# Block transposes on VectorE and two new matmul tilings in the first part of a conv-attention-MoE kernel

## The chip, the cores and the metric

The kernel runs on one core of a Trainium2 chip. The metric is the device time of one execution in microseconds (us); lower is better. Before the change the median of three runs is 6059.13 us (6056.47 to 6059.99).

A core has five engines with queues of their own, which run side by side and wait for one another by semaphores: PE (TensorE, matmuls; its weight loads are listed as PEld), DVE (VectorE), ACT (ScalarE), POOL (GpSimd) and SP (SyncE, which issues most transfers). Data lies in SBUF (128 partitions) and, for matmul results, in PSUM. Transfers between the chip's memory and SBUF are carried by 16 DMA engines. A matmul holds one operand in the array (its weights: contraction rows by output columns) and streams the other through it (the moving columns). The array can be split into tiles, for example four of 64 rows by 64 columns or four of 32 rows by 128 columns.

## The reference

`x` has the shape (32, 128, 64, 64): 32 images of 128 channels, 64 by 64 pixels, all in float32. Layer 0 adds to x a convolution in a transformed space: GroupNorm, a complex butterfly transform along H and along W, a product over channels with the transformed weights, and the inverse transforms. Layer 1 is an attention over channels and a mixture of eight experts with two chosen per pixel.

```python
def tensor_product(x, tw1, tw2, increasing_stride):
    y = jnp.swapaxes(butterfly_lastdim(jnp.swapaxes(x, -1, -2), tw1, increasing_stride), -1, -2)
    return butterfly_lastdim(y, tw2, increasing_stride)

def _kop2d(x, weight, kd1, kd2, k11, k12, k21, k22):
    xc = x.astype(jnp.complex64)
    wc = weight.astype(jnp.complex64)
    x_f = tensor_product(xc, _c(k11), _c(k12), False)
    w_f = tensor_product(wc, _c(kd1), _c(kd2), False) * math.sqrt(H * W)
    prod = jnp.einsum('bihw,oihw->bohw', x_f, w_f)
    out = tensor_product(prod, _c(k21), _c(k22), True)
    return jnp.real(out)
...
x = x + _L0_conv_ref(_gn(x), ...)
t = _to_tokens(x)
t = t + _L1_attn_ref(_ln_t(t), ...)
t = t + _L1_ffn_ref(_ln_t(t), ...)
```

The change touches only `x_f`: the GroupNorm of x and its transform along W and H. A butterfly along 64 points is a 64 x 64 complex matrix; the kernel computes the matrices once and multiplies.

## The kernel before

The kernel has three parts, one after the other. The first part takes each image through GroupNorm and the two input transforms and stores the spectrum `xf` (image, channel, w, real and imaginary h). The second part goes over the 64 columns w, mixes channels with the transformed weights and stores `pf`. The third part takes each image back, adds it to x, and does the attention and the experts.

In the first part, image b passes these steps; the names are the planner's keys and the tiles of the profile.

- `load` (L308): eight pieces of 256 KB from `x` into one of three x buffers, on SP's queue. `stats` (L315) takes the statistics of each piece on DVE. `group_norm` (L322) averages them over channel groups with two small matmuls on PE (L332, L342; tile `gps`) and small DVE steps between; `scaled` (L355) normalizes x in place in four pieces, on ACT for the first four images and on DVE after that.
- `turn_over` (L367, tile `pz`): 32 PE transposes of 128x128 per image, in four groups of eight; `turned` (L376): 16 ACT copies of 64x512 from PSUM (L383) write `z` as (w and channel half, channel, h).
- `along_w` (L389, tile `pv`): the W stage, eight groups of 32 matmuls. A matmul has 64 rows, 64 columns (all h of one channel) and 64 moving columns (`pw`, real or imaginary); four tiles of the array are used in turn. `w_out` (L402) copies each group from PSUM to `v` on ACT (L407).
- `along_h` (L413, tile `pf`): the H stage, eight groups of eight matmuls of 128 rows (h, real and imaginary), 128 columns (channels) and 128 moving columns (`ph`). `h_out` (L424) copies each group to an `f` tile, six of eight on DVE and two on ACT (L428).
- `store` (L431): two transfers of 256 KB per group, each from all 128 partitions of `f`, on SP's queue (L436).

PSUM is one pool of four tiles of two banks ("ps"), used in turn by all PE groups. There are two `z`, two `v` and four `f` buffers.

The order of the instructions is not written by hand. `Plan` (L25) simulates the engines before the kernel is built: each step has an engine, a cost in us, a due time in slots of 27.5 us (`SLOT`, L171), the steps that it comes after, and the rooms (buffers) that it takes and frees. On each engine the earliest due step that is ready and whose rooms are free goes next; the instructions are issued in that order, and each engine executes its queue in order. On PE the first part's steps keep the order in which they are added: in slot s and quarter g, the transposes of image s, two W groups of image s-1, two H groups of image s-2; the two GroupNorm matmuls of image s+1 stand before and after one quarter's W groups.

At the start DVE computes the input transform's matrices in six butterfly levels (`level`, L210) from an identity (`unit`, L198, whose copy at L204 sorts rows by parity for this layout) and copies them to `pw` and `ph` (`input_matrices`, L230).

In the second part `weights` (L617, L632; tile `g`) uses four tiles of the array of 32 rows (9 filled) by 128 columns with 128 moving columns, and takes two rooms of one kind at once; `mix` (L645, L654) follows it in turn. The second part's store (L673) reads 64 partitions.

Of the kernel before, what the change touches and what calls it, by code (L numbers as in the profile page):

```python
# [24 lines left out]
class Plan:  # L25
# [12 lines left out]
    def run(self):  # L38
# [12 lines left out]
        while True:  # L51
            for e, heap in ready.items():
                if busy[e]:
                    continue
                passed = []
                while heap:
                    due, i = heapq.heappop(heap)
                    take = ops[i][5]
                    if all(room[k] > 0 for k in take):
                        for k in take:  # L60
                            room[k] -= 1
                        order.append(i)
                        busy[e] = True
                        heapq.heappush(events, (now + ops[i][1], 0, i))
                        break
                    passed.append((due, i))
                for p in passed:
                    heapq.heappush(heap, p)
# [22 lines left out]
def kernel(  # L91
# [39 lines left out]
    pw = cp.tile([P, 2, n], F32, name="pw")  # L131
    ph = cp.tile([P, 2, n], F32, name="ph")
# [30 lines left out]
    with ExitStack() as ph1:  # L163
        pp = ph1.enter_context(tc.tile_pool(name="pp1", bufs=4, space=PSUM))
        xp = ph1.enter_context(tc.tile_pool(name="xp1", bufs=3))
        st = ph1.enter_context(tc.tile_pool(name="st1", bufs=1))
        bp = ph1.enter_context(tc.tile_pool(name="bp", bufs=1))
# [3 lines left out]
        SLOT = 27.5  # L171
# [26 lines left out]
        def unit(m, eng):  # L198
            def run():
                cur = tile_of["bf", m] = bp.tile([P, 2, n], F32, tag="bf", bufs=2, name=f"bf{m}_in")  # L200
                eng.tensor_tensor(cur[:, 0, :], ident[:, 0:n], ident[:, n : 2 * n], ALU.add)
                if m == 1:

                    eng.tensor_copy(  # L204
                        cur[lo, 0, :].rearrange("p (k r) -> p r k", r=2), ident[lo, 0:n].rearrange("p (r k) -> p r k", r=2)
                    )
                eng.memset(cur[:, 1, :], 0.0)
# [22 lines left out]
        def input_matrices():  # L230
            xa = tile_of["bf", 1]
            for half in (lo, hi):
                nc.vector.tensor_copy(pw[half], xa[hi])
            nc.vector.tensor_copy(ph[lo], xa[lo])
            nc.vector.tensor_copy(ph[hi, 1, :], xa[lo, 0, :])
            nc.vector.tensor_scalar_mul(ph[hi, 0, :], xa[lo, 1, :], -1.0)
# [130 lines left out]
        def turn_over(b, g):  # L367
            def run():
                ps = tile_of["pz", b, g] = pp.tile([P, 2, 512], F32, tag="ps", name=f"pz{b}_{g}")
                pv = ps.rearrange("w u (k c) -> w (u k) c", c=P)  # L370
                for k in range(8):
                    h = 2 * (8 * g + k)
                    nc.tensor.transpose(pv[:, k, :], xs[b][:, h * n : (h + 2) * n], ident)  # L373
            return run

        def turned(b, g, r):  # L376

            def run():
                if g == 0 and r == 0:
                    zs[b] = zp.tile([P, n, n], F32, tag="z", name=f"z{b}")  # L380
                pv = tile_of["pz", b, g].rearrange("w u (k c) -> w (u k) c", c=P)
                for half in range(2):
                    nc.scalar.copy(  # L383
                        zs[b][half * n : (half + 1) * n, :, 32 * r + 8 * g : 32 * r + 8 * g + 8],
                        pv[r * n : (r + 1) * n, :, half * n : (half + 1) * n].rearrange("w h c -> w c h"),
                    )
            return run

        def along_w(b, g):  # L389
            def run():  # L390
                ps = tile_of["pv", b, g] = pp.tile([P, 2, 512], F32, tag="ps", name=f"pv{b}_{g}")
                for k in range(8):
                    for half in range(2):
                        rows = slice(half * n, (half + 1) * n)
                        for r in range(2):
                            nc.tensor.matmul(  # L396
                                ps[r * n : (r + 1) * n, half, k * n : (k + 1) * n],
                                zs[b][rows, 8 * g + k, :], pw[rows, r, :], start=True, stop=True,
# [3 lines left out]
        def w_out(b, g):  # L402

            def run():
                if g == 0:
                    vs[b] = vp.tile([P, n, P], F32, tag="v", name=f"v{b}")
                nc.scalar.copy(  # L407
                    vs[b].rearrange("h w (a c) -> h w a c", a=2)[:, :, :, 8 * g : 8 * g + 8],
                    tile_of.pop(("pv", b, g)).rearrange("h a (c w) -> h w a c", w=n),
# [3 lines left out]
        def along_h(b, g):  # L413
            def run():
                ps = tile_of["pf", b, g] = pp.tile([P, 2, 512], F32, tag="ps", name=f"pf{b}_{g}")
                pl = ps.rearrange("c u m -> c (u m)")
                for j in range(8):
                    nc.tensor.matmul(  # L418
                        pl[:, j * P : (j + 1) * P], vs[b][:, 8 * g + j, :], ph.rearrange("h r m -> h (r m)"),
                        start=True, stop=True,  # L420
                    )
            return run

        def h_out(b, g):  # L424
            def run():
                f = tile_of["f", b, g] = fp.tile([P, 8, 2 * n], F32, tag="f", name=f"f{b}_{g}")
                copy = nc.scalar.copy if g % 4 == 3 else nc.vector.tensor_copy
                copy(f.rearrange("c w m -> c (w m)"), tile_of.pop(("pf", b, g)).rearrange("c u m -> c (u m)"))  # L428
            return run

        def store(b, g):  # L431
            def run():
                f = tile_of.pop(("f", b, g))

                for k in range(0, 8, 4):
                    nc.sync.dma_start(xf[b, :, 8 * g + k : 8 * g + k + 4, :], f[:, k : k + 4])  # L436
# [20 lines left out]
        def piece_of_image(b, k):  # L457
# [3 lines left out]
                [("pz", b - 3, g) for g in range(4)] + [("x", b, k - 1), ("pf", b - 4, k)],  # L461
# [28 lines left out]
        def piece(kind, b, g, at):  # L490
            if not 0 <= b < B:
                return
            if kind == "pz":
                add(
                    ("pz", b, g), "PE", 1.0, at, turn_over(b, g), [("nm", b, k) for k in range(4)],
                    ("ps",), ("x",) if g == 3 else (),
                )
                for r in range(2):
                    add(
                        ("zo", b, g, r), "ACT", 1.2, at, turned(b, g, r),  # L500
                        [("pz", b, g)] + [("pv", b - 2, k) for k in range(8)] + ([("zo", b, 0, 0)] if g or r else []),
                        (), ("ps",) if r else (),
                    )
            elif kind == "pv":
                add(
                    ("pv", b, g), "PE", 1.12, at, along_w(b, g),
                    [("zo", b, k, r) for k in range(4) for r in range(2)] + ["wi"], ("ps",),
                )
                add(
                    ("vo", b, g), "ACT", 1.02, at, w_out(b, g),  # L510
                    [("pv", b, g)] + [("pf", b - 2, k) for k in range(8)] + ([("vo", b, 0)] if g else []), (), ("ps",),
                )
            else:
                add(("pf", b, g), "PE", 1.95, at, along_h(b, g), [("vo", b, k) for k in range(8)], ("ps",))
                on_act = g % 4 == 3
# [9 lines left out]
        for s in range(B + 2):  # L525
            if s == 0:
                norm(2)
            for g in range(4):
# [3 lines left out]
                piece("pz", s, g, at)  # L532
                for k in range(2):
                    piece("pv", s - 1, 2 * g + k, at + 0.04 + 0.04 * k)
# [909 lines left out]
```

## Time and profile before

| | |
|---|---|
| median of three runs | 6059.13 us |
| profiled execution, its span | 6062.4 us |
| first part | 0 to 931 us |
| second part | 932 to about 2550 us |
| third part | to the end |
| PE busy over the span | 5891.6 us (97%) |
| DVE, ACT, POOL busy | 4221.2 (70%), 3756.5 (62%), 4191.0 us (69%) |

The profiled execution is its own run, 3.3 us from the median. In the page's groups and in the answers on the trace, a line reads: source line, engine, operation, output tile <- input tiles, shapes, number of records, then busy us and the mean ns of one. Matmuls overlap in the array, so the mean of one matmul is longer than the time from one start to the next; a float32 matmul has two records.

Stretches of the first part (columns: stretch in us, its length, then busy us and records of PE, PEld, DVE, ACT and POOL, the granted PE clock, the DMA engines' share and GB/s):

```profile
0.00:28.00 28.00, 6.86 (x36) 6.48 (x36) 20.94 (x91) 9.20 (x11) 3.07 (x14) 1.00 0.73 253
28.00:65.00 37.00, 24.71 (x714) 22.93 (x715) 15.59 (x33) 35.42 (x49) 1.99 (x6) 0.77 0.21 67
65.00:150.00 85.00, 83.41 (x2043) 80.00 (x2042) 46.81 (x67) 61.78 (x83) 28.51 (x80) 1.00 0.72 237
700.00:900.00 200.00, 198.35 (x4976) 190.43 (x4978) 102.83 (x140) 135.12 (x186) 12.81 (x20) 1.00 0.65 221
```

PE is busy less in the first 65 us, in which the first images pass the steps one after the other, and nearly all of the time from then on.

### The profile page before, as it was taken

The page shows a single profiled execution, that of the slowest core. Times are in us where ns is not written, and L with a number is a line of the kernel's source. Part 1 is how long each engine was busy: PE and PEld are TensorE (multiplying, and loading weights), DVE is VectorE, ACT ScalarE, POOL GpSimd, SP SyncE. Part 2 cuts the span into 40 slices and gives each one's busy share as a digit, 9 for nine tenths or more (in the row PEclk, how much of TensorE's full clock was granted, in tenths as well). Part 3 has the DMA queues.
Part 4 walks back from the last instruction along what each step waited for, and adds up shares of the span by engine and source line. Part 5 has one row for each costly group of instructions (what it writes and reads, how often), then busy time and mean ns, then how long its engine had stood idle before and what let it go on. Part 6 is the DMA issues. An engine that isn't in the chain of part 4 may idle for free.

```text
span 6062.4 us, 219265 instructions
## 1 busy us (share of the span) xinstructions
PE 5891.6 (97%) x95372; PEld 4677.6 (77%) x95372; DVE 4221.2 (70%) x7696; ACT 3756.5 (62%) x7057; POOL 4191.0 (69%) x3765
## 2 busy tenths in 40 slices
PE   7999999999999999889999999999999999999998
PEld 7999999999999999776666666666666666666654
DVE  5565545555555555448878787787878878787878
ACT  7666664555555555366667667666766766676663
POOL 2110006666666666428898898989989898998988
PEclk9999999999999999999999999999999999999999
DMA  6767666666666666632313222231322223132100
GB/s 200 238 224 237 234 214 193 172 173 172 172 174 171 171 171 172 160 107 77 92 56 102 67 88 81 72 97 57 101 68 84 84 64 104 57 97 71 65 27 28
DMA packets 555044, 756.74 MB, mean 125 GB/s; under 512 B 58592, under 2 KB 319712, under 8 KB 549984
## 3 DMA queue, kind: packets, MB, share of 16 engines
q1 hardware_dynamic: 551856, 738.76, 41.0%
q8 instruction: 749, 12.27, 0.9%
q0 software_dynamic: 896, 2.62, 0.1%
q14 instruction: 215, 1.76, 0.1%
q10 hardware_dynamic: 1328, 1.32, 0.1%
HBM read 406.93 MB, written 335.54 MB: 122 GB/s over the span
## 4 chain that ended last, share of the span: by engine, by line
PE 88%; ACT 7%; issue 2%; DVE 1%; POOL 1%; DMA 1%; SPq 0%; ACTq 0%; POOLq 0%; DVEq 0%
PE pe L1296 28%; PE m L654 17%; PE g L632 9%; PE pf L418 7%; PE pu L877 6%; PE pp L1145 4%; PE py L899 4%; PE pg L1072 4%; PE pv L396 3%; PE px L1283 2%; ACT xn L1273 2%; ACT u L887 2%; PE pz L373 1%; PE pt L1021 1%; ACT z L383 1%
## 5 line engine op out<-in xcount | busy, mean ns | idle before, releaser
L1296 PE MATMUL pe<-ew_sb,xT 128*128 128x512 f32 x4096 | 1948.4, 597 | 18.6 <-DVE tm L1307 15.1
L1307 DVE TENSOR_TENSOR tm<-pe,oh 128x512 f32<-128x512 f32 x2028 | 1346.6, 684 | 478.9 <-PE pe L1296 456.6
L1332 POOL TENSOR_TENSOR tm<-tm 128x512 f32<-128x512 f32 x1014 | 1285.0, 1284 | 202.6 <-DVE tm L1307 199.3
L1296 PEld LDWEIGHTS pe<-ew_sb,xT 128*128 128x128 f32 x4096 | 701.6, 191 | 523.4 <-issue 400.1
L643 DVE COPY f<-g 128x1024 f32<-128x1024 f32 x508 | 622.3, 1225 | 644.4 <-PE g L632 644.2
L654 PE MATMUL m<-f,s 128*64 128x64 f32 x32768 | 1068.9, 224 | 1.1 <-ACT f L643 0.8
L654 PEld LDWEIGHTS m<-f,s 128*64 128x64 f32 x32768 | 999.0, 138 | 62.4 <-issue 1.5
L600 POOL COPY s<-l 128x512 f32<-128x512 f32 x512 | 547.2, 1105 | 526.4 <-issue 509.7
L643 ACT COPY f<-g 128x1024 f32<-128x1024 f32 x508 | 514.7, 1013 | 556.4 <-PE g L632 530.1
L1335 POOL TENSOR_TENSOR tk<-tk,tm 128x256 f32<-128x256 f32 x1014 | 753.9, 743 | 79.5
L1333 POOL TENSOR_TENSOR tm<-tm 128x512 f32<-128x512 f32 x507 | 650.3, 1283 | 39.8
L887 ACT COPY u<-pu 64x512 f32<-64x512 f32 x960 | 556.3, 579 | 135.1 <-PE pu L877 121.6
L632 PE MATMUL g<-c,wst 9*128 9x128 f32 x16256 | 599.6, 283 | 1.7 <-issue 1.5
L632 PEld LDWEIGHTS g<-c,wst 9*128 9x128 f32 x16256 | 503.0, 186 | 36.2 <-issue 1.5
L349 POOL TENSOR_TENSOR grstd<-gms,mhalf 128x1 f32<-128x1 f32 x32 | 17.8, 555 | 737.8 <-DVE gms L345 737.8
L1158 ACT ACTIVATE pp<-pp,m 128x128 f32<-128x128 f32 x1024 | 440.9, 431 | 124.2 <-PE pp L1145 99.2
L602 POOL TENSOR_SCALAR s<-l 128x512 f32<-128x512 f32 x256 | 511.3, 1997 | 0.0
L877 PEld LDWEIGHTS pu<-qw,r 128*128 128x128 f32 x3840 | 455.1, 193 | 62.8 <-ACT u L887 49.0
L877 PE MATMUL pu<-qw,r 128*128 128x128 f32 x3840 | 475.8, 277 | 25.1 <-ACT u L887 25.1
L1289 ACT COPY xT<-px 128x512 f32<-128x512 f32 x256 | 150.2, 587 | 563.2 <-PE px L1283 560.1
L418 PE MATMUL pf<-ph,v 128*128 128x128 f32 x4096 | 491.2, 278 | 6.2 <-issue 1.4
L418 PEld LDWEIGHTS pf<-ph,v 128*128 128x128 f32 x4096 | 467.0, 192 | 16.0 <-ACT z L383 7.1
(169 smaller groups left out, 8569.6 us busy)
## 6 DMA issues: line engine op xcount, KB each, us to landing
xf<-f SPq DMA_DIRECT2D x512, 256.0 KB, 3.3
pf<-o SPq DMA_DIRECT2D x1024, 128.0 KB, 3.3
l<-xf SPq DMA_DIRECT2D x1012, 128.0 KB, 3.2
r<-pf SPq DMA_DIRECT2D x504, 256.0 KB, 4.7
x<-in_x_dram SPq DMA_DIRECT2D x256, 256.0 KB, 4.5
y<-in_x_dram SPq DMA_DIRECT2D x32, 2048.0 KB, 9.3
out_dram<-so SPq DMA_DIRECT2D x256, 256.0 KB, 2.2
tw<-in_tw_dram SPq DMA_DIRECT2D x6, 384.0 KB, 7.5
```

Source lines behind the costliest of these rows:

```text
L418: nc.tensor.matmul(pl[:, j * P : (j + 1) * P], vs[b][:, 8 * g + j, :], ph.rearrange("h r m -> h (r m)"), start=True, stop=True,)
L600: nc.gpsimd.tensor_copy(dst, src)
L632: nc.tensor.matmul(pg[g // 2][:, g % 2, m * P : (m + 1) * P], wst[rows, 16 * half + 4 * t + m, :], c[rows].rearrange("r h k -> r (h k)"), ...
L643: copy(f.rearrange("i m (g o) -> i m g o", g=2), tile_of["g", w, half, t][k].rearrange("i g (o m) -> i m g o", o=4))
L654: nc.tensor.matmul(ps[hh * n : (hh + 1) * n, q, :], s[:, h].rearrange("i k b -> i (k b)")[:, B * r : B * r + n], f[:, h, r, :], start=(r = ...
L877: nc.tensor.matmul(ps[:, k, :], rs[b, e][:, k * P : (k + 1) * P], qw.rearrange("w r m -> w (r m)"), start=True, stop=True,)
L887: nc.scalar.copy(u[r * n : (r + 1) * n, :, oh * n + 8 * e : oh * n + 8 * e + 8], ps[oh * n : (oh + 1) * n, :, r * n : (r + 1) * n].rearran ...
L1296: nc.tensor.matmul(ps, tile_of["xT", b, i // 4][:, i % 4, :], ew_sb[:, es, :].rearrange("d e c -> d (e c)"), start=True, stop=True,)
L1307: nc.vector.tensor_tensor(tile_of["tm", b, i // 2][:, i % 2, es, :], tile_of.pop(("pe", b, i, half)).rearrange("p (e c) -> p e c", c=P), t ...
L1332: nc.gpsimd.tensor_tensor(tm[:, k, 0:4, :], tm[:, k, 0:4, :], tm[:, k, 4:8, :], ALU.add)
L1333: nc.gpsimd.tensor_tensor(tm[:, :, 0:2, :], tm[:, :, 0:2, :], tm[:, :, 2:4, :], ALU.add)
L1335: nc.gpsimd.tensor_tensor(t[:, lo : lo + 2, :], t[:, lo : lo + 2, :], tm[:, :, m, :], ALU.add)
```

## The change

The PE transposes and their copies go. In their place DVE transposes x in blocks of 32x32, four instructions of 128x1024 per image: within each group of 32 partitions, 32 channels by 32 pixels of a row are turned. `z` becomes (w of a half row and channel quarter, half u, channel, h).

The W stage multiplies four tiles of 32 rows by 128 columns, one per channel quarter q, with two channels of 64 h as the columns and 128 moving columns (real and imaginary m); the two halves u of a row are accumulated. A group is 32 matmuls, writes two PSUM tiles and takes two rooms; there are four groups per image instead of eight. `w_out` copies the same number of tiles to `v`, whose partitions are now (channel of the pair, h).

The H stage multiplies tiles of 64x64: 64 rows (h of one channel of the pair), 64 columns (channel pairs), 128 moving columns; real and imaginary parts are accumulated. A group is 32 matmuls instead of eight. `h_out` puts six of eight copies on ACT and two on DVE. A store reads 64 partitions (one value of t) with two channels each; there are two per group, of 256 KB, as before.

The matrices `pw` and `ph` have two more copies of their halves, move from the constant pool to a pool of the first part, and are filled by 14 small copies instead of five. The row sort in `unit` goes. In the planner, a step that takes two rooms of a kind now needs two free ones, the slot is 23.0 us, and the costs are restated.

```diff
-                    if all(room[k] > 0 for k in take):
+                    if all(room[k] >= take.count(k) for k in take):
...
-    pw = cp.tile([P, 2, n], F32, name="pw")
-    ph = cp.tile([P, 2, n], F32, name="ph")
...
+        pw = st.tile([P, 2, 2, n], F32, name="pw")
+        ph = st.tile([P, 2, 2, n], F32, name="ph")
...
-        SLOT = 27.5
+        SLOT = 23.0
...
-                if m == 1:
-
-                    eng.tensor_copy(
-                        cur[lo, 0, :].rearrange("p (k r) -> p r k", r=2), ident[lo, 0:n].rearrange("p (r k) -> p r k", r=2)
-                    )
...
+            for q in range(4):
+                for half in range(2):
+                    nc.vector.tensor_copy(pw[32 * q : 32 * q + 32, half], xa[n + 32 * half : n + 32 * half + 32])
             for half in (lo, hi):
-                nc.vector.tensor_copy(pw[half], xa[hi])
-            nc.vector.tensor_copy(ph[lo], xa[lo])
-            nc.vector.tensor_copy(ph[hi, 1, :], xa[lo, 0, :])
-            nc.vector.tensor_scalar_mul(ph[hi, 0, :], xa[lo, 1, :], -1.0)
+                nc.vector.tensor_copy(ph[half, 0], xa[lo])
+                nc.vector.tensor_copy(ph[half, 1, 1, :], xa[lo, 0, :])
+                nc.vector.tensor_scalar_mul(ph[half, 1, 0, :], xa[lo, 1, :], -1.0)
...
-        def turn_over(b, g):
...
-                    nc.tensor.transpose(pv[:, k, :], xs[b][:, h * n : (h + 2) * n], ident)
...
+        def turned(b, k):
...
+                    zs[b] = zp.tile([P, 2, 32, n], F32, tag="z", name=f"z{b}")
+                nc.vector.transpose(
+                    out=zs[b][:, :, :, 16 * k : 16 * k + 16].rearrange("w u c h -> w h u c"),
+                    in_=xs[b][:, k * 1024 : (k + 1) * 1024].rearrange("c (h u w) -> c h u w", u=2, w=32),
+                )
...
         def along_w(b, g):
...
+                ps = [pp.tile([P, 2, 512], F32, tag="ps", name=f"pv{b}_{g}_{k}") for k in range(2)]
+                tile_of["pv", b, 2 * g], tile_of["pv", b, 2 * g + 1] = ps
+                for k in range(4):
+                    lo = 8 * g + 2 * k
+                    for u in range(2):
+                        for q in range(4):
+                            rows = slice(32 * q, 32 * q + 32)
                             nc.tensor.matmul(
-                                ps[r * n : (r + 1) * n, half, k * n : (k + 1) * n],
-                                zs[b][rows, 8 * g + k, :], pw[rows, r, :], start=True, stop=True,
+                                ps[q // 2][:, q % 2, k * P : (k + 1) * P],
+                                zs[b][rows, u, lo : lo + 2, :].rearrange("w c h -> w (c h)"),
+                                pw[rows, u].rearrange("w r m -> w (r m)"), start=(u == 0), stop=(u == 1),
                             )
...
         def along_h(b, g):
...
-                for j in range(8):
-                    nc.tensor.matmul(
-                        pl[:, j * P : (j + 1) * P], vs[b][:, 8 * g + j, :], ph.rearrange("h r m -> h (r m)"),
-                        start=True, stop=True,
-                    )
+                for j in range(4):
+                    for r in range(2):
+                        for t in range(2):
+                            for a, half in enumerate((lo, hi)):
+                                nc.tensor.matmul(
+                                    ps[t * n : (t + 1) * n, a, j * P : (j + 1) * P],
+                                    vs[b][half, r * n + 32 * t + 4 * g + j, :],
+                                    ph[half, r].rearrange("h s m -> h (s m)"), start=(r == 0), stop=(r == 1),
+                                )
...
-                copy = nc.scalar.copy if g % 4 == 3 else nc.vector.tensor_copy
+                copy = nc.vector.tensor_copy if g % 4 == 3 else nc.scalar.copy
...
-                for k in range(0, 8, 4):
-                    nc.sync.dma_start(xf[b, :, 8 * g + k : 8 * g + k + 4, :], f[:, k : k + 4])
+                for t in range(2):
+                    w = 32 * t + 4 * g
+                    nc.sync.dma_start(
+                        xf[b].rearrange("(c a) w m -> c a w m", a=2)[:, :, w : w + 4, :], f[t * n : (t + 1) * n]
+                    )
...
-                    ("pz", b, g), "PE", 1.0, at, turn_over(b, g), [("nm", b, k) for k in range(4)],
...
+                    ("zo", b, g), "DVE", 1.8, at, turned(b, g),
+                    [("nm", b, g), ("zo", b, g - 1)] + [("pv", b - 2, k) for k in range(4)], (), ("x",) if g == 3 else (),
...
+                add(("pv", b, g), "PE", 1.9, at, along_w(b, g), [("zo", b, k) for k in range(4)] + ["wi"], ("ps", "ps"))
...
-                add(("pf", b, g), "PE", 1.95, at, along_h(b, g), [("vo", b, k) for k in range(8)], ("ps",))
-                on_act = g % 4 == 3
+                add(("pf", b, g), "PE", 1.85, at, along_h(b, g), [("vo", b, k) for k in range(8)], ("ps",))
+                on_act = g % 4 != 3
...
-                piece("pz", s, g, at)
-                for k in range(2):
-                    piece("pv", s - 1, 2 * g + k, at + 0.04 + 0.04 * k)
+                piece("zo", s, g, at)
+                piece("pv", s - 1, g, at + 0.04)
```

## The prediction

> **What bounds the kernel now.** I read the stretches first, then the first part's engine timelines, its groups, its waits and its DMA. The stretch of one image in the quiet middle of the first part (columns: stretch, length, then busy us and instructions of PE, PEld, DVE, ACT, POOL, granted clock, DMA share, GB/s):
>
> ```profile
> 550.00:577.40 27.40, 27.29 (x689) 26.27 (x683) 15.94 (x23) 18.88 (x27) 0.55 (x1) 1.00 0.73 242
> ```
>
> PE is busy 27.29 of 27.40 us at full clock; DVE, ACT and the DMA engines have room. So each image costs what PE needs for it. The PE timeline there, one quarter of an image (start, us, line, tile), and two places of the second part that show a shape the change will use:
>
> ```profile
> 562.31 1.04 PE L373 MATMUL pz<-ident,x 128*128 128x128 f32 x8
> 563.27 2.10 PE L396 MATMUL pv<-pw,z 64*64 64x64 f32 x128
> 565.30 3.84 PE L418 MATMUL pf<-ph,v 128*128 128x128 f32 x32
> 568.98 1.04 PE L373 MATMUL pz<-ident,x 128*128 128x128 f32 x8
> ...
> 932.46 1.17 PE L632 MATMUL g<-c,wst 9*128 9x128 f32 x32 [1.19 <-issue]
> 933.43 1.10 PE L632 MATMUL gm<-c,wst 9*128 9x128 f32 x32
> ...
> 955.38 1.17 PE L632 MATMUL g<-c,wst 9*128 9x128 f32 x32
> 956.48 2.08 PE L654 MATMUL m<-f,s 128*64 128x64 f32 x64
> ```
>
> From start to start: transposes 0.96, W group pair 2.03, H group pair 3.68, together 6.67 us, four times 26.7. The GroupNorm matmuls fill the rest, 27.45 - 26.7 = 0.75 per image (H stage starts at 565.30 and 592.80, 27.5 apart). An f32 matmul has two records, so the 128 records of W are 64 matmuls and the 32 of H are 16.
>
> **What the change removes from PE.** The 32 transposes per image, 4 x 0.96 = 3.84 us. They lie on the path: nothing else runs on PE meanwhile.
>
> **W stage.** 64 matmuls of 64x64 tiles with 64 moving columns per quarter become 32 matmuls of 32x128 tiles with 128. The row nearest to it is L632: four row groups of the array, 128 weight columns, 128 moving columns, each group into its own bank. 16 such matmuls take 1.10 us with a change of shape behind them (955.38 to 956.48) and 0.97 when more of the same follow (932.46 to 933.43). So 32 take 0.97 + 1.10 = 2.07 us. Lower bound 2 x 0.97 = 1.94, upper 2 x 1.10 = 2.20. I take 2.07: against 2.03 now, practically unchanged, although twice the number is streamed per matmul. That L632 fills 9 rows of 32 and W all 32 is the difference that I can't price; the moving columns and the weight columns are the same.
>
> **H stage.** 16 matmuls of 128x128 per pair become 64 of 64x64 tiles with 128 moving columns, accumulated over two halves. In the records the 16 run at one record per 112 ns; the four tiles of W's 64x64 shape start within 20 ns of one another, and a set of four repeats every 58 ns for 64 columns; L632's set of four at 128 columns repeats every 112 ns. So four 64x64 tiles at 128 columns should repeat every 112: 64 matmuls x 2 records / 4 x 0.112 = 3.58, plus 0.10 for the change of shape, 3.68 as now. Upper bound: everything in W's shape doubles, 2 x 2.03 = 4.06. I take 3.70.
>
> PE per image: 4 x (2.07 + 3.70) + 0.75 = 23.8 us against 27.45.
>
> **DVE.** It gets four transposes per image and gives four of its six PSUM copies to ACT. Its groups and worst wait over 200 to 900 us:
>
> ```profile
> L428 DVE COPY f<-pf 128x1024 f32<-128x1024 f32 x152 | 182.6, 1216 | 116.5 <-PE pf L418 107.4 <-ACT v L407 3.9 <-DMA xf<-f 2.3
> L319 DVE BATCH_NORM_STATS2 gbs<-x 128x6 f32<-128x512 f32 x185 | 121.1, 684 | 91.8 <-DMA x<-in_x_dram 91.6
> L362 DVE TENSOR_SCALAR x<-x,gms,grstd 128x1024 f32<-128x1024 f32 x96 | 74.6, 840 | 17.2 <-POOL grstd L349 17.2
> L383 ACT COPY z<-pz 64x512 f32<-64x512 f32 x399 | 231.4, 580 | 133.2 <-PE pz L373 129.6
> L407 ACT COPY v<-pv 128x1024 f32<-128x1024 f32 x203 | 195.7, 1015 | 6.6 <-PE pv L396 4.2
> ...
> DVE gbs L319 <- DMA x<-in_x_dram: 91.6, 49, 3.7
> ```
>
> Statistics 8 x 0.684 = 5.5, scaling 4 x 0.84 = 3.4, two copies 2.4, small GroupNorm steps 1.1: 12.4 us plus four transposes of 128x1024. No block transpose is in the trace. From below: a 128x1024 pass between SBUF tiles, 0.84. From above, the slowest plain f32 pass of the page, POOL's 1997 ns for 512 elements (L602), 4.0 for 1024. The nearest is DVE's own 1024-element PSUM copy, 1.22; with an output written at a stride of 64 elements I take 1.8, halfway from it to its double. Then DVE has 12.4 + 7.2 = 19.6 us of an image, plus 91.6 / 25 images = 3.7 in which the in-order queue stands at a statistics instruction whose x has not landed: 23.3 of 23.8. The cover is thin but there; transposed data is wanted a full step later, so the transposes themselves are hidden.
>
> [...]
>
> **ACT** loses 16 x 0.58 = 9.3 us of L383 and gains 4 x 1.01 of L428: 8.1 + 6.1 = 14.2 us per image, 60%. Where L407 and L428 follow each other, a W group's two PSUM tiles are free 0.2 + 2 x 1.02 + 0.2 = 2.4 us after its end, and the next W group comes after 3.7: no wait of PE, 1.3 us of cover.
>
> **DMA.** Bytes and issues stay (8 loads, 16 stores, 256 KB each), but a store now reads 64 partitions instead of 128. The DMA view over 300 to 500 us:
>
> ```profile
> DMA packets 24683, 45.53 MB, mean 228 GB/s; under 512 B 2743, under 2 KB 2743, under 8 KB 24639
> q1 hardware_dynamic: 24639, 44.85, 66.8%
> xf<-f SPq DMA_DIRECT2D x112, 256.0 KB, 3.3
> ```
>
> 66.8% of 16 x 200 us over the 21,896 packets of 2 KB is 97 ns each (the packet records: median 84). In the second part the 2 KB packets are the pf stores from 64 partitions, and their records have a mean of 136 ns, median 147, beside 512-byte loads at 28. Half the partitions, dearer packets. Per image now: 3072 x 97 / 16 = 18.6 us of DMA. After: 2048 stores x 140 and 1024 loads x 97, over 16: 24.1 us; bounds 18.6 (nothing changes) and 2048 x 154 + 1024 x 97, over 16 = 25.9. That is as much as PE's 23.8. Two resources that are both full, with four f buffers between them and loads behind stores in one SP queue, do not overlap perfectly: I take a period of 25.0 us. What is late first is a store; then its f buffer, then ACT's copy behind it, then PE for a PSUM tile; a late x holds DVE at L319, then the two copies and the GroupNorm steps behind it, and PE at the second GroupNorm matmul.
>
> [...]
>
> **Start, end, the rest.** Now the first H group starts at 61.78 and the last ends at 931.3 us: 32 x 14.7 + 31 x 8.1 + 30 x 3.84 + 26 for GroupNorm and weights = 863 of PE work in 869.5. After, DVE has the twiddles done at 25.8 + 1.8 (nine more small copies at 0.2), then four transposes and perhaps image 1's statistics (4.9): 35 to 40; W of image 0 takes 8.3, its copies 2.4: first H group at 46 to 51, I take 49. The dropped copy at L204 (0.24) is nothing. The planner's count of rooms touches besides W only the second part's L632 groups, which take two rooms; there PE is busy 500.0 of 500 us, each group follows a mix of 2 us and both rooms are free by then: 0, at most 8 x 1.25 = 10 us at its first column. The new SLOT only orders.
>
> **Sum.** Last H group at 49 + 31 x 25.0 + 14.8 + 3 = 842 us against 931: -89 in the profiled execution, whose span 6062.4 is 3.3 above the runs' median 6059.1. So 6059 - 89 = 5970.
>
> **Rivals.**
> - PE alone sets the end: packets stay near 97 ns because loads and stores interleave. 49 + 31 x 23.8 + 15 + 8 = 810, -121: 5938, to 5925 with W at 1.94. For it: today's share of 0.68 leaves room. Against: the 136 ns.
> - DMA, or waits that it causes, goes deeper: packets at 154, or the two DVE copies stuck behind a late x (3.7 us against 2.3 of cover, twice an image). Period 26 to 27.7: 6000 to 6053.
> - Slower: the block transpose is far slower than a copy and DVE becomes the bound. At 4.0 us: 12.4 + 3.7 + 16 = 32.1 per image, 49 + 31 x 32.1 + 18 = 1062, +131: 6190. It decides from (27.45 - 16.1) / 4 = 2.8 us per transpose on. Against it: 2.3 times the PSUM copy for the same elements.
> - The gain is eaten exactly, period 27.5 to 27.9: 6047 to 6071.
>
> **Chances.** Forecast, period 24.2 to 26: 0.47, own range 5948 to 6000. PE alone 0.24; deeper 0.15; eaten 0.04; slower 0.10. A measurement tells from no change about 0.2%, 12 us. Faster 0.87, same 0.03, slower 0.10. The range 5925 to 6035 leaves out about 0.2.
>
> **What would show it.** No pz group on PE; W groups at 2.07 and H pairs at 3.7 from start to start; DVE transposes near 1.8 and below 2.8; first H group near 49; the DMA share near 0.95 in the first part with 2 KB packets well over 97 ns, and PE waiting about 1.2 us per image on copies that wait for stores or for x. Packets unchanged, or a transpose above 2.8, would make the prediction wrong; so would H tiles that don't run four at a time (a pair near twice 3.7).

## The result, and the profile after

The changed kernel took 6082.86 us (median of five runs, 6074.96 to 6087.64) against 6059.13: ratio 1.0037, 95% interval 1.0024 to 1.0049. It became slower by 0.4% where 5970 was forecast. Ratios compare runs at the usual granted clock: one run of the kernel before (6686.03 us, clock 0.846) and one of tall_h below (9293.08 us, 0.585) are left out of them. The profiled span grew from 6062.4 to 6083.8 us, and as much lies in the first part: the second part's first matmul starts at 954.65 us instead of 932.46, 22.2 us later. From 1000 to 2450 us PE is busy for 1449.4 us before and 1449.6 after.

The same stretches as before, and the one image in the middle (columns as before):

```profile
0.00:28.00 28.00, 1.14 (x4) 1.00 (x4) 20.75 (x96) 5.92 (x5) 3.08 (x14) 1.00 0.72 253
28.00:65.00 37.00, 14.59 (x304) 14.05 (x308) 30.88 (x44) 16.32 (x16) 1.98 (x6) 0.91 0.20 65
65.00:150.00 85.00, 78.10 (x2336) 72.70 (x2332) 52.21 (x62) 46.01 (x47) 28.86 (x80) 0.94 0.75 220
550.00:577.40 27.40, 24.54 (x719) 22.49 (x713) 17.49 (x22) 12.78 (x13) 0.55 (x1) 0.94 0.77 226
700.00:900.00 200.00, 182.05 (x5580) 167.11 (x5573) 125.43 (x151) 99.46 (x101) 13.37 (x21) 0.99 0.78 221
```

Until 65 us PE does less than before (304 records against 714 in the second line): the first H group starts at 65.88 us, not at 61.78. After that PE is no longer full: 24.54 of 27.40 us where it was 27.29, 182.05 of 200 where it was 198.35. Nothing else is full either. ACT is down as meant, DVE is at 63%, the DMA engines at 0.78. So the first part is no longer bound by any engine's work.

The PE timeline: the start, an undisturbed stretch, and the middle (the bracket is the idle time before the line and what released it):

```profile
47.03 0.59 PE L329 MATMUL gps<-gmv,gmean 128*128 128x1 f32 x2 [9.77 <-DVE gmv L325]
47.55 3.55 PE L385 MATMUL pv<-pw,z 32*128 32x128 f32 x64
...
60.07 5.87 PE L385 MATMUL pv<-pw,z 32*128 32x128 f32 x124 [4.55 <-ACT v L398]
65.88 3.72 PE L411 MATMUL pf<-ph,v 64*64 64x128 f32 x128
...
72.30 3.72 PE L411 MATMUL pf<-ph,v 64*64 64x128 f32 x128
75.96 2.07 PE L385 MATMUL pv<-pw,z 32*128 32x128 f32 x64
77.95 3.72 PE L411 MATMUL pf<-ph,v 64*64 64x128 f32 x128
...
568.95 1.88 PE L411 MATMUL pf<-ph,v 64*64 64x128 f32 x38 [2.06 <-issue]
570.76 3.09 PE L385 MATMUL pv<-pw,z 32*128 32x128 f32 x64
573.78 3.72 PE L411 MATMUL pf<-ph,v 64*64 64x128 f32 x128
577.44 1.15 PE L385 MATMUL pv<-pw,z 32*128 32x128 f32 x26
579.18 1.39 PE L385 MATMUL pv<-pw,z 32*128 32x128 f32 x38 [0.59 <-issue]
580.50 2.83 PE L411 MATMUL pf<-ph,v 64*64 64x128 f32 x90
584.30 1.32 PE L411 MATMUL pf<-ph,v 64*64 64x128 f32 x38 [0.96 <-issue]
```

From 72.30 the step runs as priced: H pair 75.96 - 72.30 = 3.66 us, W group 1.99. In the middle PE pauses with the releaser "issue": the profile shows no semaphore, engine or buffer that it waited for. The pauses come inside groups, and their distance is fixed in records, not in work. From 568.95 to 579.18 there are 38 + 64 + 128 + 26 = 256 matmul records, from 579.18 to 584.30 38 + 90 = 128.

The groups over 200 to 900 us (PEld is the weight loads; last come idle time and its releasers):

```profile
L411 PE MATMUL pf<-ph,v 64*64 64x128 f32 x12776 | 402.4, 272 | 45.6 <-issue 43.9 <-DVE f L422 1.1
L411 PEld LDWEIGHTS pf<-ph,v 64*64 64x64 f32 x12777 | 359.8, 133 | 73.8 <-issue 62.6 <-DVE f L422 1.8
L385 PE MATMUL pv<-pw,z 32*128 32x128 f32 x6336 | 222.8, 281 | 19.1 <-issue 19.0
...
L369 DVE STREAM_TRANSPOSE z<-x 128x1024 f32<-128x1024 f32 x100 | 194.9, 1952 | 48.8 <-PE pv L385 48.8
L398 ACT COPY v<-pv 128x1024 f32<-128x1024 f32 x200 | 192.7, 1015 | 247.9 <-PE pv L385 247.9
...
L316 DVE BATCH_NORM_STATS2 gbs<-x 128x6 f32<-128x512 f32 x188 | 125.4, 673 | 92.5 <-DMA x<-in_x_dram 92.3
```

DVE and ACT wait for PE (L369, L398), and PE's two groups wait for "issue": 43.9 + 19.0 us of the 700. A late copy of the H stage (L422) costs PE 1.1 us in all. The DMA view over 300 to 500 us:

```profile
q1 hardware_dynamic: 24903, 45.36, 76.9%
q8 instruction: 43, 0.70, 1.5%
xf<-f SPq DMA_DIRECT2D x115, 256.0 KB, 4.1
```

The line that explains the pauses is the small one. 43 packets with 0.70 MB are packets of 16,384 bytes. Over the whole execution PE has 98,444 matmul records, as many weight loads and 838 waits and drains, together 772.4 times 256, and q8 has 772 packets, each of 16,384 bytes: one for 256 instructions of PE. Such 256 instructions, 128 matmul records and their weight loads, are called a chunk below. Set beside the pauses (worked out from the trace's records, in us):

```
instruction packet starts   lands     PE resumes   after landing
566.57                      567.53    568.95       1.42
576.93                      577.81    579.18       1.37
581.86                      582.74    584.30       1.56
587.52                      588.46    589.82       1.36
```

From 200 to 780 us 95 distances between matmul starts exceed 250 ns, 85.7 us together; they are called pauses below. (PE is busy for 520.26 us of these 580, so some 60 us of idle time lie in them.) 86 of them, 79.3 us, end 1.2 to 1.75 us after such a packet has landed; by chance 12% would. In PE's instruction count 85 of the 95 stand at 193 or 194 modulo 256. So the reading at this point was: PE has run out of instructions and waits for the next 256.

The granted clock is another candidate, since the line of 550 to 577.40 us has 0.94. It stood at 0.5 for 3.4 or 6.8 us at five places between 65 and 950 us, 20.5 us together, which is at most 10 us of PE's work. Each place begins within 1.4 us of the end of a distance of 2.1 to 3.1 us between two matmul starts. Slot28 (below) has no such place from 65 to 955 us and pauses just as much, so the clock does not make the pauses.

### The profile page after: what moved, and what is told of

Read it like the earlier page. It is cut to its first block, busy times and chain, and to the rows that moved or that the text cites. A ratio compares the mean times of both kernels' runs of the same rounds, so it can differ in the third digit from the quotient of the medians.

```text
span 6083.8 us, 224918 instructions
## 1 busy us (share of the span) xinstructions
PE 5816.3 (96%) x98444; PEld 4570.8 (75%) x98444; DVE 4300.1 (71%) x7704; ACT 3592.6 (59%) x6673; POOL 4191.5 (69%) x3765
## 4 chain that ended last, share of the span: by engine, by line
PE 88%; ACT 5%; issue 2%; DVE 2%; DMA 1%; POOL 1%; SPq 0%; ACTq 0%; POOLq 0%; DVEq 0%
PE pe L1284 28%; PE m L642 17%; PE g L620 9%; PE pf L411 8%; PE pu L865 6%; PE pv L385 4%; PE pp L1133 4%; PE py L887 4%; PE pg L1060 4%; PE px L1271 2%; ACT xn L1261 2%; ACT u L875 2%; PE pt L1009 1%; PE po L1330 1%; ACT tk L1014 1%
## 5 line engine op out<-in xcount | busy, mean ns | idle before, releaser
L1284 PE MATMUL pe<-ew_sb,xT 128*128 128x512 f32 x4096 | 1947.9, 597 | 18.5 <-DVE tm L1295 15.4
L411 PE MATMUL pf<-ph,v 64*64 64x128 f32 x16384 | 516.2, 273 | 61.8 <-issue 57.7
L411 PEld LDWEIGHTS pf<-ph,v 64*64 64x64 f32 x16384 | 464.0, 134 | 95.9 <-issue 79.4
L346 POOL TENSOR_TENSOR grstd<-gms,mhalf 128x1 f32<-128x1 f32 x32 | 17.8, 555 | 751.5 <-DVE gms L342 722.6
```

What stands on the lines that cost most here:

```text
L411: nc.tensor.matmul(ps[t * n : (t + 1) * n, a, j * P : (j + 1) * P], vs[b][half, r * n + 32 * t + 4 * g + j, :], ph[half, r].rearrange("h s ...
L1284: nc.tensor.matmul(ps, tile_of["xT", b, i // 4][:, i % 4, :], ew_sb[:, es, :].rearrange("d e c -> d (e c)"), start=True, stop=True,)
```

## The experiments

Three theories, numbered as the expectations number them. Theory 1: PE waits for its own instructions, and their packets come late because of the data transfers, above all the stores from half the partitions. Theory 2: PE waits for its instructions beside any such traffic, because an image now has 772 matmul records instead of 676 (the four of GroupNorm included) for less work. Theory 3: not the instructions, but the planner's new order and slot, or the buffers. Periods below are (start of the last H record - start of the first) / 32, which is 27.16 us before and 27.66 after. Where no ratio is given, the time is that of one run.

**full_store.** Stores read all 128 partitions again; matmuls as in the changed kernel. The spectrum's layout in memory changes with it, and so does the second part's load.

```diff
-                for t in range(2):
-                    w = 32 * t + 4 * g
+                for a in range(2):
                     nc.sync.dma_start(
-                        xf[b].rearrange("(c a) w m -> c a w m", a=2)[:, :, w : w + 4, :], f[t * n : (t + 1) * n]
+                        xf[b, :, :, a, 4 * g : 4 * g + 4, :].rearrange("t c w m -> (t c) w m"), f[:, a]
```

> The changed kernel with xf laid out as (image, t, channel pair, a, w, m), so that each of the two stores of a group reads all 128 partitions again; bytes, packet size and the number of transfers are the same, and the second part reads the same columns from the new places. Theory 1 (PE stands because its instructions, fetched in 16 KB packets of 128 matmul records by the same DMA engines, come late behind the long packets of stores from 64 partitions): 2 KB packets back to a mean near 97 ns from 110, PE's pauses of over 250 ns between 200 and 900 us from 98.6 us to under 30, period per image from 28.0 to 24.5 us, time near 5975. Theory 2 (the fetch can't keep up with 128 records in 3.7 us beside any such traffic): pauses 80 to 100 us, period 27.5 to 28, time 6070 to 6085. Theory 3 (DVE or PSUM order, not the fetch): no change, 6075 to 6085.

Measured: 6059.99 us, ratio to before 1.0001 (0.9991 to 1.0011); period 26.54; the mean 2 KB packet 97.9 ns, after 110 to 112. Most of the pauses stayed: 69.3 us from 200 to 780 us (after: 85.7). This lies between what theories 1 and 2 named. The stores are a part, 1.1 us of an image, not the main cause. The time hides some of the gain: the second part starts 31.2 us earlier (923.44 us), but from its first matmul to its last mix it takes 1609.9 us instead of 1604.2; its loads read the spectrum from the new layout, but no run shows whether that is why.

**before_half.** The kernel before, with its stores made from 64 partitions.

> The kernel before with its stores cut in halves of 64 partitions (four transfers of 128 KB per group instead of two of 256 KB, packets of 2 KB as before). Theory 1: 2 KB packets rise from 97 to about 125 ns and PE's pauses rise, but a packet of instructions is wanted only every 5.2 us there: time 6065 to 6100. Theory 2: 6055 to 6065, since neither the records nor their rate change. Theory 3: 6055 to 6065.

Measured: 6163.63 us, far outside all three. The edit doubled the stores to four of 128 KB per group, 727 issues on SP in 700 us at about 0.6 us, and x came late: DVE stood 266 us for x. This priced SP's queue, not the partitions.

**wide_h.** One H matmul streams 256 columns: half the instructions for the same columns.

```diff
-                    for r in range(2):
-                        for t in range(2):
+                    for t in range(2):
...
-                                    vs[b][half, r * n + 32 * t + 4 * g + j, :],
-                                    ph[half, r].rearrange("h s m -> h (s m)"), start=(r == 0), stop=(r == 1),
+                                vs[b][half, 32 * t + 4 * g + j, :],
+                                ph[half].rearrange("h r s m -> h (r s m)"), start=True, stop=True,
```

> The changed kernel with an H group of 16 matmuls of 256 moving columns instead of 32 of 128: the sum over the imaginary half is left out and half of the output columns are overwritten. The columns streamed, the PSUM copies and the transfers stay; PE's records per image fall from 768 to 512. Theories 1 and 2: a packet of instructions lasts 5.8 us instead of 3.9, pauses under 25 us between 200 and 900 us, period 23.5 to 24.5, time 5955 to 5985. Theory 3: as in the changed kernel, period 28, time 6075 to 6085.

Measured: 5951.25 us, period 23.36, both slightly below what theories 1 and 2 named, with the stores still from 64 partitions and the DMA engines at 0.87, more than after has. Wide_h over 200 to 780 us, first the stretch, then the H stage's group:

```profile
200.00:780.00 580.00, 568.85 (x12640) 429.92 (x12638) 443.99 (x548) 335.56 (x341) 56.91 (x135) 1.00 0.87 267
```

```profile
L410 PE MATMUL pf<-ph,v 64*64 64x256 f32 x6272 | 361.8, 379 | 1.6 <-DVE f L421 1.6
```

No "issue" at the H groups any more. PE stands idle for 11.2 of the 580 us. Transfers that keep the DMA engines at 0.87 do not hold this kernel back, which the prediction's DMA term said they would.

**slot28.** SLOT 28.0 instead of 23.0, nothing else.

> The changed kernel with the planner's slot at 28.0 us, near the period that was measured, instead of 23.0: only the due times differ. Theories 1 and 2: the fetch decides, period 27.5 to 28.5, time 6070 to 6095. Theory 3 (the order planned for 23 us makes DVE and PE wait for each other): period 25 to 27, time 5990 to 6050.

Measured: 6090.66 us, period 27.80, pauses from 200 to 900 us of 113.1 us (after: 98.6). Slot28 over 200 to 780 us:

```profile
200.00:780.00 580.00, 509.85 (x15552) 463.23 (x15553) 385.40 (x473) 277.71 (x283) 52.41 (x138) 1.00 0.79 226
```

The slot of 23.0 is not the cause, and, with the clock at 1.00 in the whole stretch, neither is the clock.

**half_stores.** As full_store, with only every second group stored (`for a in range(2 if g % 2 == 0 else 0)`).

> full_store with the stores of every second H group left out; the second part reads the columns that were stored in their place, so half of the spectrum is missing. PE's instructions stay as in the changed kernel (768 records per image), DMA bytes of the first part fall by a third. Theory 1 (data transfers delay the instruction fetch): PE's pauses between 200 and 900 us fall from 78.8 to under 35 us, first part to about 66 + 32 x 24 = 835 us, time near 5975. Theory 2 (a fetch of 256 instructions takes some 4.4 us by itself, longer than the 3.7 to 3.9 us that PE needs for them): pauses 65 to 85 us, time 6035 to 6060.

Measured: 6032.88 us, period 25.84. Half_stores over 200 to 780 us, the stretch and the H stage's group:

```profile
200.00:780.00 580.00, 538.96 (x16838) 494.46 (x16841) 409.09 (x511) 300.33 (x305) 53.37 (x140) 1.00 0.52 165
```

```profile
L411 PE MATMUL pf<-ph,v 64*64 64x128 f32 x11146 | 348.9, 272 | 38.4 <-issue 36.7 <-DVE f L422 1.1
```

With the DMA engines at 0.52, where full_store has 0.73, 60.8 of full_store's 69.3 us of pauses are left. That spoke for theory 2. But the mean share hides that 80 of some 130 chunks still began beside busy engines, as the table of the last run below shows, so this run does not settle how far traffic matters.

**tall_h, tall_h_full.** The H stage as two tiles of 64 rows by 128 columns: two w of the same half in one matmul. 32 matmul records of an H group instead of 64, for the same sums.

```diff
-                        for t in range(2):
-                            for a, half in enumerate((lo, hi)):
+                        for a, half in enumerate((lo, hi)):
+                            w = r * n + 8 * g + 2 * j
...
-                                    ps[t * n : (t + 1) * n, a, j * P : (j + 1) * P],
-                                    vs[b][half, r * n + 32 * t + 4 * g + j, :],
+                                ps[:, a, j * P : (j + 1) * P],
+                                vs[b][half, w : w + 2, :].rearrange("h t c -> h (t c)"),
```

tall_h stores from 64 partitions, tall_h_full from 128.

> The changed kernel with the H stage in two tiles of 64 rows by 128 columns: the columns are two neighbouring w with 64 channel pairs, so one matmul does what two 64x64 ones did; xf is laid out as (image, parity of w, pair, a, w/2, m), stores still read 64 partitions. Same columns streamed per tile, same copies and bytes, PE's records per image 512 instead of 768, nothing left out. Theories 1 and 2 (instruction fetch): as wide_h, pauses under 60 us of which under 10 end with a fetch, period 23.4 to 24, time 5945 to 5965. If it were the 64x64 shape or a waiting copy, period 27 to 28, time over 6040.

> tall_h with each store reading 128 partitions. Theory 1: what pauses are left go as well, 5 to 15 us below tall_h. Theory 2: with the fetch no longer in the way the packets of the stores are hidden, within 5 us of tall_h.

Measured: tall_h 5976.52 us, ratio 0.9859 (0.9842 to 0.9875), period 23.83, a time above what was expected (from its first matmul to its last mix the second part takes 1613.2 us, in the changed kernel 1604.2); tall_h_full 5963.56, ratio 0.9841 (0.9825 to 0.9858), period 23.54. Both have the same layout of the spectrum and differ in the stores alone. Of the 13 us between them 6.3 arise in the first part, where the stores are (the second part's first matmul at 832.59 and 826.31 us); the rest comes later, where the code is the same, and is not explained by the partitions. The PE timeline of tall_h:

```profile
409.90 3.84 PE L411 MATMUL pf<-ph,v 64*128 64x128 f32 x64
413.67 2.07 PE L385 MATMUL pv<-pw,z 32*128 32x128 f32 x64
415.67 3.84 PE L411 MATMUL pf<-ph,v 64*128 64x128 f32 x64
```

Half the instructions take 413.67 - 409.90 = 3.77 us, hardly more than the 3.66 of the 64x64 tiles. PE gains nothing at work, and the pauses are nearly gone (12.2 us in tall_h, 3.1 in tall_h_full). Tall_h_full over 200 to 780 us:

```profile
200.00:780.00 580.00, 578.30 (x12532) 552.78 (x12532) 441.50 (x545) 333.96 (x340) 56.35 (x134) 1.00 0.81 265
```

**tall_h_start, tall_h_best.** tall_h_full, with the GroupNorm matmuls of image 2 put behind more of image 0's W groups: `if g == (2 if s == 1 else min(s, 3) - 1)`. Both are the same kernel; the first was timed once, the second four times.

> tall_h_full with the two GroupNorm matmuls of image 2 added behind the third W group of image 0 instead of before and after the first. In the changed kernel the first of them waits until 47.0 us for image 2's statistics, while the transposed image 0 is ready at 40.2 us. If that matmul holds the start: first W group at 40 to 41 us, first H group 5 to 8 us earlier than in tall_h_full, time 4 to 8 us below it. If ACT's copies and scaling hold it: first H group unmoved, same time within 2 us.

> tall_h_start again, now timed in rounds: 5948 to 5958, 8 to 12 us below tall_h_full's 5963.6, from the first H group at 59.5 instead of 66.6 us.

The PE timeline of tall_h_start:

```profile
40.17 5.92 PE L385 MATMUL pv<-pw,z 32*128 32x128 f32 x128 [3.01 <-DVE z L369]
...
59.51 6.46 PE L411 MATMUL pf<-ph,v 64*128 64x128 f32 x64 [4.45 <-ACT v L398]
```

The first W group starts at 40.17 instead of 47.81 us and the first H group at 59.51 instead of 66.55: the start moved by 7 us. The times are 5953.14 in the one run and 5960.07 as the median of four (ratio 0.9836, 0.982 to 0.9853), slightly above what was expected. Of the 7 us 4.2 reach the end of the last H group (815.84 against 820.00 us). The last interval overlaps tall_h_full's, so the gain is shown in the trace, not in the times.

**tall_1of4.** Only two of eight H groups get tall tiles, by full_store's stores: 704 records per image. If the shape of the tile cost time, a quarter of the gain should come; if the fetch of instructions bounds until PE's own work is longer, most of it.

> tall_h_full with only every fourth H group in tiles of 64x128 and the others in 64x64: 704 records of PE per image between 512 (tall_h_full, period 23.5 us) and 768 (full_store, 26.5 us). If PE gets 128 records (256 instructions) per 4.4 to 4.5 us at best, the measured loop: 5.5 x 4.45 = 24.5 us per image, time 5985 to 6005. If the 64x64 shape is slow by itself, three quarters of the difference: 25.8 us, time 6030 to 6040.

Measured: 5996.47 us, period 24.46, pauses 18.5 us. A quarter of the edit brings 2.08 of the 3.00 us of period from full_store to tall_h_full. That fits a floor that is passed as the instructions get fewer, and not a cost per tile.

**before_4col.** The kernel before, with each H matmul cut into four tiles of 128 rows by 32 columns: about 1060 records per image, no block transpose, stores from all partitions.

> The kernel before with each H matmul of 128x128 cut in four of 128 rows by 32 columns, which stand in the array side by side and stream the same 128 columns; nothing else of the change. Records per image rise from 676 to about 1060. If instruction fetch is the bound at 4.4 to 4.5 us per 128 records: period 36 to 38 us instead of 27.3, time 6340 to 6410, with pauses of PE every 256 instructions. If the count of instructions does not matter (the cause lies in the new data paths): 6055 to 6090.

Measured: 6315.83 us, period 35.0, slightly less than expected. The PE timeline:

```profile
563.84 2.09 PE L396 MATMUL pv<-pw,z 64*64 64x64 f32 x128
565.86 1.50 PE L420 MATMUL pf<-ph,v 128*32 128x128 f32 x45
569.29 2.59 PE L420 MATMUL pf<-ph,v 128*32 128x128 f32 x83 [1.93 <-issue]
```

More instructions for the same sums put the same pauses into the old kernel: 94 of its 104 pauses from 200 to 780 us end 1.2 to 1.75 us after a packet of instructions, and 97 stand at 193 or 194 modulo 256, with neither a block transpose nor a store from half the partitions.

**eighth_stores.** full_store with only group 0 of each image stored, to tell a fetch of fixed time from one that stands behind data.

> As half_stores, but seven eighths of the spectrum's stores are left out (only group 0 of each image is stored, and the second part reads it in place of the others), so the first part's transfers fall to the eight loads per image and two stores; all 256 KB stores that are left read 128 partitions. PE's instructions are those of full_store. Theory 'the fetch itself has a fixed time': the mean interval of a chunk of 256 PE instructions stays where half_stores had it, 4.3 to 4.4 us, PE's pauses of 200 to 780 us at 50 to 65 us, period 25.4 to 25.9, time 6015 to 6035. Theory 'the fetch is slow because its packets stand behind data packets': share of the DMA engines near 0.3, the interval falls to 4.0 to 4.2 us (what PE's own work takes), pauses under 25 us, period 24.0 to 24.9, time 5975 to 6005. In between the two shares are read from the interval.

Measured: 5996.15 us, period 24.57, the mean interval of a chunk 4.13 us, pauses 26.9 us, a little over what the second theory named and far below the first's. The stretch from 200 to 780 us and PE's groups in it:

```profile
200.00:780.00 580.00, 560.96 (x17990) 525.26 (x17985) 433.94 (x541) 321.11 (x326) 46.73 (x119) 0.99 0.34 111
```

```profile
L411 PE MATMUL pf<-ph,v 64*64 64x128 f32 x11914 | 355.6, 272 | 7.7 <-issue 6.0 <-DVE f L422 1.4
L385 PE MATMUL pv<-pw,z 32*128 32x128 f32 x5952 | 200.1, 279 | 10.7 <-issue 10.7
```

With 0.34 of the DMA engines in use the same 768 records run nearly without pauses. Sorting each chunk of 256 PE instructions by what the DMA engines carried in its first 2 us (worked out from the records, 200 to 780 us):

```
kernel          engines busy   chunks   start of chunk to   chunk,
                                        fetch, median us    mean us
eighth_stores   under 0.2      81       0.88                3.89
half_stores     under 0.2      35       1.13                3.96
eighth_stores   0.6 and more   42       2.06                4.67
half_stores     0.6 and more   80       2.26                4.67
after           0.6 and more   112      2.23                4.73
```

The transfer of the 16 KB itself takes 0.95 to 1.1 us in all of them, and PE starts 1.4 us after it. Under traffic: 2.2 + 1.0 + 1.4 = 4.6 us for 256 instructions. Without it: 0.9 + 1.1 + 1.4 = 3.4, less than the 3.7 to 3.9 that PE needs to execute them (3.66 us for an H pair's 128 records, 3.89 for eighth_stores' mean quiet chunk). So most of the pauses in this kernel need both: many instructions for little work, and busy DMA engines. The delay lies before the packet starts, not in its transfer; what holds it there, the records do not show.

## Why the prediction was wrong

**PE's work** was right. W groups take 1.99 us (2.07 predicted), H pairs 3.66 (3.70); four tiles of 64x64 do run at once: in the pair at 72.30 us four records start within 20 ns of one another, and sets of four are 111 ns apart on average. The sum of 23.8 us per image is what tall_h (23.83) and wide_h (23.36) come to. The rival "PE alone" had this period; it did not come because PE has to wait for its instructions.

**DVE and ACT** were right. A block transpose takes 1.95 us (1.8 predicted) and is hidden: DVE waits 48.8 us for PE at it. The slow-transpose rival named the direction, slower, but for a reason that did not hold, so its agreement is luck.

**The step that failed is the period in the DMA part**, "Two resources that are both full ... I take a period of 25.0 us". It priced transfers by their data only: late store, f buffer, ACT, PSUM tile, PE. Next to none of that reached PE: ACT waited 12.0 us of 700 for stores at L422, PE 1.1 us at L411. The 2 KB packets grew to 110 to 112 ns on average, not to the 126 that 140 and 97 make, and the engines' share to 0.78, not to 0.95. With the same bytes and stores from 64 partitions tall_h ran at 23.83 and wide_h, which leaves out a sum but no transfer, with the engines at 0.87, at 23.36, both below the 24.1 of the DMA term. What sets the period is a term that the sum lacks, and so put at nothing without a reason: the fetch of PE's instructions. An image has 768 + 4 matmul records, 6.03 chunks of 256 instructions, and at 4.6 us that is 27.7; measured 27.66. (From 200 to 780 us the packets are 4.68 us apart on average, which makes 28.2 there.) Before it was 676 / 128 x 4.6 = 24.3, below PE's work of 27.2, so the fetch hardly showed (from 200 to 780 us 4.2 us of pauses end 1.2 to 1.75 us after a packet has landed, against 79.3 after); tall_h's 516 need 18.5. The 4.6 us belong to this traffic: before_4col, with the engines at 0.55, has its packets 4.31 us apart. The traffic that the prediction feared does enter, but by delaying instructions: full_store's quicker packets give back 1.1 us per image.

Two rivals held the measured period: "deeper" (26 to 27.7) and "eaten exactly" (27.5 to 27.9). The first rested on packets of 154 ns or on copies stuck behind a late x, and the packets averaged 110 to 112 ns and PE lost 1.1 us of 700 to late copies; the second named no cause. So both agree by luck.

**The start** was mis-sized: 49 us predicted for the first H group, 65.88 measured. Image 0 was turned at about 40 us, but in PE's order the GroupNorm matmul of image 2 stood ahead of its first W group and waited 9.77 us for DVE; then the W groups waited 4.55 us for the copies on ACT, which stood behind 4.63 us of scaling (L357). The last two W groups took 5.81 us (60.07 to 65.88) where two take 4.0 later on; the granted clock from 60 to 66 us was 0.64. Adding up work and copies left out the order of the queues and the clock. This is 17 us of the miss, of which tall_h_start got 7 back.

**The sum.** Last H group 950.86 against 842: 17 from the start and 32 x (27.66 - 25.0) = 85 from the period make 102 of the 109 us; the other 7 are the last image, taken at 14.8 + 3 us instead of a whole period of 25.0. Two lesser sums of the prediction do not come out. W at 1.94 us gives 5922, not 5925. A period of 27.9 gives 49 + 31 x 27.9 + 17.8 = 932 and a time of 6060, not 6071. Neither carries the forecast.

## What to carry to other kernels

Count instructions, not only their time: where 128 matmul records and their weight loads took less than 4.3 to 4.7 us beside the transfers of this first part (4.31 is the mean distance of the packets in before_4col, 4.73 a chunk's mean in the changed kernel under traffic), PE waited for its own code; the profile calls it "issue", and it comes at a fixed distance in instructions (after: 85 of 95 pauses at 193 or 194 modulo 256). Look for that sign rather than for the number: the second part had no such pauses at 4.16 us (see below). A tiling that does the same work in fewer matmuls (64x128 instead of two of 64x64) then gains although no matmul is faster (3.77 us for tall_h's 64 records, 3.66 for the 128 of 64x64): tall_h_full and tall_h_best beat both kernels, at 0.984 of the time before. And at the start of a pipeline read the order of the queue, not the sum of the work.

## What was not expected of the hardware

PE's instructions come during execution, in packets of 16,384 bytes that the profile counts among those of the 16 DMA engines (q8, 772 of them in the changed kernel); by the medians of the table above the next fetch starts 0.9 to 1.1 us after the start of a chunk in quiet stretches (eighth_stores, half_stores) and 2.1 to 2.3 us after it in busy ones (these two and the changed kernel). In the second part, however, chunks of 4.16 us show hardly a pause (two over 250 ns from 1000 to 2450 us, 0.8 us together) though the engines are busy for 0.66 of the time; there the fetch starts about 0.65 us after the start of the chunk. Its packets are mostly of 512 bytes (237,568 from 1000 to 2450 us, beside 59,610 of 2 KB); whether that is why stays open.
